# Two rows of a sample to a partition, four 64x64 tiles, the residual in the matrices, output slots and half stores

## The chip, the cores and the metric

The kernel runs on one core of one Trainium2 chip. The time is that of one execution on the device, in microseconds (us). Before the change it is 323.08 us, the median of three runs (323.06 to 323.25).

## What is computed

Each of 128 samples is a matrix of 128 channels by 1024 steps (float32, 512 KB). It is multiplied by the one of eight 128x128 matrices that its subject index names, and added to the product.

```python
B, C, D, T, N_SUBJECTS = (128, 128, 128, 1024, 8)
...
w = weights[subjects]
out = jnp.einsum('bct,bcd->bdt', x, w)
...
x = x + _L0_cond_ref(x, itok_B_0_7, L0_cond_weights)
```

67 MB come in, 67 MB go out, and everything is float32.

## The kernel before

A *turn* is four samples, two *halves* (`H`) of two samples (`G`); there are 32 turns. Twelve slots in SBUF (`xs`, pieces of `x_all`) hold one turn each: channel c of a sample stands in partition c, 4 KB of it, and the four samples stand side by side, 16 KB in a partition. A slot is loaded, overwritten with the sums, and stored.

The work is written for each engine by hand, between semaphores:

- **ACT's queue** issues the loads (`load`, through `transfer`, L67), one for each sample. `ROWS` = 4 makes the reading side one run of four rows, 16 KB; the writing side is four pieces of 4 KB in four partitions. A load waits only until its slot is stored (`s_slot`); the twelfth waits until the weights are sorted, since its slot holds them at first.
- **SP's queue** loads the weights (L192) and the indices (L195), then issues the stores (L251 for turn 0, `store` through L67 for the others). A store takes a whole turn from 128 partitions, 16 KB each; in the output these are four rows of 4 KB. The last twelve turns are stored in pairs (`PAIR`), the last six in runs of 32 KB (`WHOLE`). A store waits for the sums of its turn (`s_added`), and between turns `EARLY` = 8 and 24 for those of `BEHIND` = 4 turns more.
- **TensorE** runs a loop of 32 turns (`multiply`, L174): for each half four matmuls of 128x128 by 512 columns into that half's four banks of PSUM (`ps`). It waits for the two matrices (`s_go`) and for the landed samples (`s_ready`, L170). Ahead of the loop three matmuls on zeros (`IDLE`, L200) fill the time.
- **VectorE** sorts the weights at the start (two transposes, L208 and L227, and twelve of the sixteen copies at L230). Its loop then waits for a half's products, adds them to the samples in the slot (`add`, L186, 128x2048), and copies the two matrices of the next turn into place (`place`, L165), at addresses from the subject indices, which it loads into registers once a turn (L154).
- **GpSimd** does four of the sorting copies (L230) and then turns landed loads into `s_ready`.

Of the kernel before, what the change touches and what calls it, by code (L numbers as in the profile page):

```python
# [30 lines left out]
G = 2  # L31
H = 2

N = 512

SLOTS = 12

P_SLOTS = 2

BEHIND = 4  # L40
# [4 lines left out]
PAIR = 2  # L45
WHOLE = 6

DMA = 16

SORTED = 18  # L50

IDLE = 3
# [28 lines left out]
def kernel(  # L81
# [10 lines left out]
    NT = B // (G * H)  # L92
# [4 lines left out]

    room = -(nc.sbuf_base + -nc.sbuf_base % 32) % ALIGN
    if room:
        sbuf("room", C, room // 4)  # L100
    x_all = sbuf("x_all", C, SLOTS * H * G * T)
    xs = [
        x_all[:, i * H * G * T : (i + 1) * H * G * T].rearrange("c (q t) -> c q t", t=T)
        for i in range(SLOTS)
    ]
    w_all = sbuf("w_all", C, S, D)
    w_raw, w_mid, w_late = (xs[SLOTS - 1][:, q, :] for q in range(3))
    ws = [sbuf(f"w{i}", C, 1, D) for i in range(H * G)]
    zeros = sbuf("zeros", C, N)
    given, near, wrap = (sbuf(name, 1, B, dtype=I32) for name in ("given", "near", "wrap"))  # L110
    index = sbuf("index", 1, B + H * G, dtype=I32)
    ps = [
        ctx.enter_context(nc.psum_tensor(f"ps{i}", [D, G, T], F32)).ap() for i in range(P_SLOTS)
# [5 lines left out]
    s_zeros = tc.alloc_semaphore("s_zeros")  # L119
    s_product = tc.alloc_semaphore("s_product")  # L120
    s_added = tc.alloc_semaphore("s_added")

    s_ready = tc.alloc_semaphore("s_ready")
    s_go = tc.alloc_semaphore("s_go")

    s_slot = [tc.alloc_semaphore(f"s_slot{k}") for k in range(SLOTS)]
    s_head = tc.alloc_semaphore("s_head")
    s_sort = tc.alloc_semaphore("s_sort")

    def emptied(i):  # L130
        turns = i // SLOTS
        return DMA * (H * G + 1) * turns - (DMA * G if i >= SLOTS and i % SLOTS == 0 else 0)

    def load(engine, i, q):
# [17 lines left out]

    def subjects_of(i):
        _, subject = nc.values_load_multi_w_load_instructions(  # L154
            index[0:1, i] if isinstance(i, slice) else index[0:1, bass.ds(i * (H * G), H * G)],
            engines=[mybir.EngineType.DVE],
            min_val=0,
            max_val=S - 1,
            skip_runtime_bounds_check_because="the index is clamped on the chip above",
        )  # L160
        return subject

    def place(h, subject):
        for q in range(h * G, (h + 1) * G):
            copy = nc.vector.tensor_copy(ws[q], w_all[:, bass.ds(subject[q], 1), :])  # L165
        copy.then_inc(s_go, 1)

    def multiply(slot, h):
        nc.tensor.wait_ge(s_go, 1).then_inc(s_go, -1)
        nc.tensor.wait_ge(s_ready, 1).then_inc(s_ready, -1)  # L170
        for q in range(h * G, (h + 1) * G):
            for t in range(0, T, N):
                at = slot * (H * G * T) + (q * T + t)
                mm = nc.tensor.matmul(  # L174
                    ps[h][:, q % G, t : t + N],
                    ws[q][:, 0, :],
                    x_all[:, bass.ds(at, N)],
                    start=True,
                    stop=True,
                )  # L180
        mm.then_inc(s_product, 1)

    def add(slot, h):
        mine = x_all[:, bass.ds(slot * (H * G * T) + h * G * T, G * T)]
        nc.vector.wait_ge(s_product, 1).then_inc(s_product, -1)  # L185
        nc.vector.tensor_tensor(  # L186
            mine, ps[h].rearrange("d g t -> d (g t)"), mine, ALU.add
        ).then_inc(s_added, 1)

    with tc.tile_critical():  # L190

        nc.sync.dma_start(  # L192
            w_raw, weights.rearrange("s (u j) d -> (s u) (j d)", j=S)
# [5 lines left out]
        for _ in range(IDLE):  # L199
            nc.tensor.matmul(  # L200
                ps[P_SLOTS - 1][:, G - 1, :N], zeros[:, :D], zeros, start=True, stop=True
            )

        nc.vector.wait_ge(s_wall, DMA)
        nc.vector.transpose(  # L208
            w_mid.rearrange("p (e h w j) -> p j h e w", e=S, h=4, w=4), w_raw
        ).then_inc(s_sort, 1)  # L210
        nc.vector.memset(index[:, B:], 0).then_inc(s_index, 1)  # L211
# [5 lines left out]
        nc.vector.tensor_tensor(index[:, :B], near, wrap, ALU.add).then_inc(s_index, 1)  # L217
        for i in range(NT):
            if i == SLOTS - 1:
                nc.scalar.wait_ge(s_sort, SORTED)  # L220
            if i >= SLOTS:
                nc.scalar.wait_ge(s_slot[i % SLOTS], emptied(i))
            for q in range(H * G):
                load(nc.scalar, i, q)

        nc.vector.wait_ge(s_sort, 1)
        nc.vector.transpose(w_late, w_mid).then_inc(s_sort, 1)  # L227

        def sort(engine, o, v):
            engine.tensor_copy(  # L230
                w_all[32 * v : 32 * (v + 1), 2 * o : 2 * (o + 1), :],
                w_late[32 * o : 32 * (o + 1)].rearrange("c (e v d) -> c v e d", v=4, d=D)[:, v],
            ).then_inc(s_sort, 1)

        nc.vector.wait_ge(s_sort, 2)
        nc.gpsimd.wait_ge(s_sort, 2)
        for o in range(4):
            for v in range(4):
                sort(nc.gpsimd if v == 3 else nc.vector, o, v)
        for i in range(NT):  # L240
            if i == 0:
                nc.gpsimd.wait_ge(s_head, DMA * G).then_inc(s_ready, 1)
                nc.gpsimd.wait_ge(s_slot[0], DMA * G).then_inc(s_ready, 1)
            else:
                nc.gpsimd.wait_ge(s_slot[i % SLOTS], emptied(i) + DMA * H * G).then_inc(s_ready, H)

        for i in [*range(NT - SLOTS), *range(NT - SLOTS, NT, PAIR)]:
            n = 1 if i < NT - SLOTS else PAIR
            nc.sync.wait_ge(s_added, (i + n + (BEHIND if EARLY <= i < NT - LAST else 0)) * H)
            if i == 0:  # L250
                nc.sync.dma_start(  # L251
                    out[: H * G].rearrange("g d t -> d g t"), xs[0]
                ).then_inc(s_slot[0], DMA)
            elif i + n < NT:
                store(i, n).then_inc(s_slot[i % SLOTS], DMA)


        nc.vector.wait_ge(s_index, 4)
        nc.vector.wait_ge(s_sort, SORTED)
# [50 lines left out]
```

## Time and profile before

| | |
|---|---|
| time, median of three runs | 323.08 us |
| span of the profiled execution, first to last instruction | 320.9 us |
| moved by DMA | 134.76 MB, mean 420 GB/s |
| TensorE busy | 248.9 us, 78% |
| VectorE busy | 172.6 us, 54% |
| GpSimd busy | 1.9 us, 1% |
| mean granted TensorE clock | 0.893 |

The profiled execution has no time of its own beside its span; what lies around the span is taken as the difference to the runs' median. Times in the profile count from the start of the span. A row of the groups reads: line, engine, operation, output<-input, count, then busy time and the mean ns of one, then the engine's idle time just before them and what ended most of it. SPq and ACTq are the sequencers that issue DMAs. A busy TensorE is not TensorE at its peak, since its matmuls are pipelined and the records overlap.

### The profile page before, as it was taken

The numbers are of one execution on the slowest core, as the hardware profiler recorded it, in microseconds if no ns is written. First come the engines' busy times: TensorE is split into PE (matmuls) and PEld (weight loads), VectorE is DVE, ScalarE is ACT, GpSimd is POOL, SyncE is SP. The second block draws the span as 40 slices with busy tenths as digits, with TensorE's granted clock in tenths as the row PEclk, the third lists the DMA queues.
The fourth block names the chain that finished last, engine by engine and source line by source line (L and its number), as shares of the span: only waits on it lengthen the run. The fifth ranks groups of instructions, "written<-read, shape, count | busy, mean of one in ns | idle before, by whom it ended". The sixth has DMA issues, their size and how long they took to land. (4 is left out here: it accounts for less than half of the span.)

```text
span 320.9 us, 2386 instructions
## 1 busy us (share of the span) xinstructions
PE 248.9 (78%) x518; PEld 102.8 (32%) x518; DVE 172.6 (54%) x216; POOL 1.9 (1%) x8
## 2 busy tenths in 40 slices
PE   6199999999997699998498469988599957874000
PEld 2134444444433244443133224333244422331000
DVE  4636776777676167775435362675367745066000
POOL 0200000000000000000000000000000000000000
PEclk9679999999999599999789797999799989599555
DMA  7999999999999999999999999999999999999996
GB/s 294 425 425 412 426 423 432 429 423 425 425 425 425 425 424 425 425 429 425 429 435 431 427 427 429 425 425 425 425 425 425 425 425 425 427 427 455 429 445 274
DMA packets 10803, 134.76 MB, mean 420 GB/s; under 512 B 2481, under 2 KB 2482, under 8 KB 3122
## 3 DMA queue, kind: packets, MB, share of 16 engines
q1 hardware_dynamic: 4658, 67.64, 49.7%
q10 hardware_dynamic: 6144, 67.12, 49.6%
q14 instruction: 1, 0.01, 0.0%
HBM read 67.63 MB, written 67.11 MB: 420 GB/s over the span
## 5 line engine op out<-in xcount | busy, mean ns | idle before, releaser
L174 PE MATMUL ps<-x_all,w 128*128 x512 | 243.8, 635 | 42.0 <-PEq L170 34.3
L186 DVE TENSOR_TENSOR x_all<-ps,x_all 128x2048 f32 x64 | 146.7, 2292 | 117.3 <-DVEq L185 117.3
L174 PEld LDWEIGHTS ps<-x_all,w 128*128 128x128 f32 x512 | 100.9, 203 | 185.2 <-issue 184.6
L165 DVE COPY w<-w_all 128x128 f32 x132 | 23.2, 219 | 0.8 <-DVE w_all L230 0.8
L200 PE MATMUL ps<-zeros 128*128 128x512 f32 x6 | 5.2, 1033 | 1.7 <-DVE zeros L197 1.7
L230 DVE COPY w_all<-x_all 32x256 f32<-32x256 f32 x12 | 3.9, 326 | 0.4
L208 DVE STREAM_TRANSPOSE x_all<-x_all 128x1024 f32<-128x1024 f32 x1 | 2.0, 1992 | 3.1 <-DMA x_all<-in_L_cond_weights_dram 3.1
L200 PEld LDWEIGHTS ps<-zeros 128*128 128x128 f32 x6 | 1.8, 328 | 3.7 <-issue 2.1
L230 POOL COPY w_all<-x_all 32x256 f32<-32x256 f32 x4 | 1.7, 425 | 8.3 <-DVE x_all L227 8.1
L227 DVE STREAM_TRANSPOSE x_all<-x_all 128x1024 f32<-128x1024 f32 x1 | 1.2, 1225 | 0.0
L197 DVE MEMSET zeros<- 128x512 f32 x1 | 0.5, 485 | 1.0 <-SPq L190 1.0
L217 DVE CUSTOM_DVE_ANT_0 index<-near,wrap 1x256 uint16<-1x256 uint16 x1 | 0.3, 280 | 0.0
L215 DVE TENSOR_SCALAR wrap<-near 1x128 int32<-1x128 int32 x1 | 0.2, 215 | 0.0
L213 DVE TENSOR_SCALAR near<-given 1x128 int32<-1x128 int32 x1 | 0.2, 205 | 0.0
L297 POOL MEMSET const-bfloat16-1.0<- 128x1 bf16 x1 | 0.1, 100 | 0.0
L297 POOL MEMSET const-float32-0.0<- 128x1 f32 x1 | 0.1, 98 | 0.2 <-issue 0.2
L297 POOL MEMSET const-uint8-127<- 128x1 uint8 x1 | 0.1, 98 | 0.0
L297 POOL MEMSET const-float32-1.0<- 128x1 f32 x1 | 0.1, 97 | 0.0
L297 DVE BASE_LOAD x1 | 0.0, 21 | 0.1
L211 DVE MEMSET index<- 1x4 int32 x1 | 0.1, 62 | 0.0
## 6 DMA issues: line engine op xcount, KB each, us to landing
x_all<-in_x_dram ACTq DMA_DIRECT2D x128, 512.0 KB, 34.2
out_dram<-x_all SPq DMA_DIRECT2D x20, 2048.0 KB, 18.3
out_dram<-x_all SPq DMA_DIRECT2D x6, 4096.0 KB, 30.3
x_all<-in_L_cond_weights_dram SPq DMA_DIRECT2D x1, 512.0 KB, 3.7
given<-in_itok_B_dram SPq DMA_DIRECT2D x1, 0.5 KB
```

The costliest lines, as they stand in the source:

```text
L165: copy = nc.vector.tensor_copy(ws[q], w_all[:, bass.ds(subject[q], 1), :])
L174: mm = nc.tensor.matmul(ps[h][:, q % G, t : t + N], ws[q][:, 0, :], x_all[:, bass.ds(at, N)], start=True, stop=True,)
L186: nc.vector.tensor_tensor(mine, ps[h].rearrange("d g t -> d (g t)"), mine, ALU.add).then_inc(s_added, 1)
L197: nc.vector.memset(zeros, 0.0).then_inc(s_zeros, 1)
L200: nc.tensor.matmul(ps[P_SLOTS - 1][:, G - 1, :N], zeros[:, :D], zeros, start=True, stop=True)
L208: nc.vector.transpose(w_mid.rearrange("p (e h w j) -> p j h e w", e=S, h=4, w=4), w_raw).then_inc(s_sort, 1)
L213: nc.vector.tensor_scalar(near, given, -S, S - 1, ALU.max, ALU.min).then_inc(s_index, 1)
L215: nc.vector.tensor_scalar(wrap, near, 0, S, ALU.is_lt, ALU.mult).then_inc(s_index, 1)
L217: nc.vector.tensor_tensor(index[:, :B], near, wrap, ALU.add).then_inc(s_index, 1)
L227: nc.vector.transpose(w_late, w_mid).then_inc(s_sort, 1)
L230: engine.tensor_copy(w_all[32 * v : 32 * (v + 1), 2 * o : 2 * (o + 1), :], w_late[32 * o : 32 * (o + 1)].rearrange("c (e v d) -> c v e d", ...
L297: nc = _bacc.Bacc("TRN2", target_bir_lowering=False, num_devices=1)
```

## The change

*Layout.* A sample now takes 64 partitions with two of its rows in each, 8 KB, and two samples fill the 128 partitions. A turn is still four samples: two such pairs (`P`), each of two samples (`H`).

*Loads.* One load brings a pair: 64 runs of 16 KB on the reading side, two pieces of 8 KB each on the writing side. There are four input slots (`IN`), and a load waits until the sums of the turn four before it are copied out (`s_added`).

*Products.* A matrix is split by even and odd rows and columns into four 64x64 parts. A product is 32 calls of 64x64 by 512 columns, in four blocks `b` of eight; four calls in a row have their four tiles (`tile`: input rows `h`, output partitions `h ^ p`) in different quarters of the array. The identity (`same`, made by two selects on GpSimd) is added to each matrix as it is placed, so the product is the sum already. Both pairs together fill PSUM; blocks 0 and 2 write its first half, 1 and 3 the second. Blocks 0 and 1 wait until their half is copied out (`s_free`).

*Sums.* VectorE copies the products, a pair and a half of PSUM at a time (128x1024), into eight output slots (`OUT`). It waits for a free one (`s_room`), which GpSimd signals from the stores. Matrices are placed two turns ahead, into two sets.

*Stores.* By the crossing of tiles, partitions 0 to 63 of an output slot hold samples 0 and 3 of the turn, and 64 to 127 samples 1 and 2. So each half of the partitions is stored by itself: 64 runs of 16 KB, two pieces of 8 KB each in the output. `BEHIND` is 3.

*Start.* The weights are loaded by ACT's queue, ahead of the samples, 1 KB at a time into 64 partitions; one copy on VectorE and two parts of another, on VectorE and GpSimd (`SHARE` = 6 of 8), sort them. There are five matmuls on zeros.

On TensorE, the loop over turns before, with the waits (`ps` is PSUM, `w` the placed matrices; the ISA rows set an address):

```order
6 L174 ISA [waits s_go,s_ready]
7 L174 MATMUL ps<-x_all,w 128x512
8 L174 ISA
9 L174 MATMUL ps<-x_all,w 128x512
10 L174 ISA
11 L174 MATMUL ps<-x_all,w 128x512
12 L174 ISA
13 L174 MATMUL ps<-x_all,w 128x512
14 L174 ISA [waits s_go,s_ready]
```

And after, the first turn of the four in the loop's body and the start of the next:

```order
6 L192 MATMUL ps<-x_in,w 64x512 [waits s_go,s_ready,s_free]
7 L192 MATMUL ps<-x_in,w 64x512 x7
8 L192 MATMUL ps<-x_in,w 64x512 [waits s_free]
9 L192 MATMUL ps<-x_in,w 64x512 x23
10 L192 MATMUL ps<-x_in,w 64x512 [waits s_go,s_ready,s_free]
```

A turn's eight calls have become 32 smaller ones, the address rows are gone, and the two waits by half a turn have become one for landed data and two for free PSUM.

On VectorE, one turn of the loop before:

```order
23 L154 TENSOR_LOAD index
24 L186 ISA [waits s_product]
25 L186 TENSOR_TENSOR x_all<-ps,x_all 128x2048
26 L165 ISA
27 L165 COPY w<-w_all 128x128
28 L165 ISA
29 L165 COPY w<-w_all 128x128
30 L186 ISA [waits s_product]
```

And one turn after:

```order
29 L157 TENSOR_LOAD index
30 L204 ISA [waits s_room,s_product]
31 L204 COPY x_out<-ps 128x1024
32 L204 ISA
33 L204 COPY x_out<-ps 128x1024
34 L204 ISA [waits s_product]
35 L204 COPY x_out<-ps 128x1024
36 L204 ISA
37 L204 COPY x_out<-ps 128x1024
38 L168 ISA
39 L168 TENSOR_TENSOR w<-w_all,same 64x256
```

The additions have become copies, all four placements of a turn now stand behind its last copy, and a wait for an output slot stands in front.

On ACT's queue, the loads before:

```order
2 L67 DMA x_all<-in_x_dram 128x1024 x44
3 L67 DMA x_all<-in_x_dram 128x1024 [waits s_sort]
4 L67 DMA x_all<-in_x_dram 128x1024 x3
5 L67 DMA x_all<-in_x_dram 128x1024 [waits s_slot0]
6 L67 DMA x_all<-in_x_dram 128x1024 x3
```

And after:

```order
2 L67 DMA x_out<-in_L_cond_weights_dram 64x8x256
3 L67 DMA x_in<-in_x_dram 128x2048 x8
4 L67 DMA x_in<-in_x_dram 128x2048 [waits s_added]
5 L67 DMA x_in<-in_x_dram 128x2048
6 L67 DMA x_in<-in_x_dram 128x2048 [waits s_added]
```

44 loads of a sample went out without a wait, 22 MB; now it is the weights and eight loads of a pair, 8.4 MB, and each further turn waits for sums.

The core of the diff:

```diff
-SLOTS = 12
-P_SLOTS = 2
-BEHIND = 4
+IN = 4
+OUT = 8
+BEHIND = 3
...
-IDLE = 3
+IDLE = 5
+SHARE = 6
...
-    def store(i, n):
-        at = i % SLOTS * H * G * T
+    def load(i, p):
+        at = (i % IN * P + p) * SIZE
+        first = i * Q + p * H
         transfer(
             nc,
-            engine,
-            xs[i % SLOTS][:, q, :],
-            x[i * H * G + q].rearrange("(a r) t -> a (r t)", r=ROWS),
-        ).then_inc(s_head if i * H * G + q < G else s_slot[i % SLOTS], DMA)
+            nc.scalar,
+            x_in[:, at : at + SIZE],
+            x[first : first + H].rearrange("h (b r) t -> (h b) (r t)", r=ROWS),
+        ).then_inc(s_in[i % IN], DMA)
+    def store(i, h):
+        at = i % OUT * P * SIZE
+        first, step = (i * Q + h, Q - 1 - 2 * h)
         return transfer(
             nc,
             nc.sync,
-            out[i * H * G : (i + n) * H * G].rearrange("g d t -> d g t"),
-            x_all[:, at : at + n * H * G * T].rearrange(
-                "d (o t) -> d o t", o=1 if i >= NT - WHOLE else n
-            ),
+            out[first : first + step + 1 : step].rearrange("p (a r) t -> a p (r t)", r=R),
+            x_out[h * A : (h + 1) * A, at : at + P * SIZE].rearrange("a (o f) -> a o f", o=1),
         )
...
+    def place(u, subject):
+        return [
+            nc.vector.tensor_tensor(
+                ws[u][p][h * A : (h + 1) * A],
+                w_all[h * A : (h + 1) * A, bass.ds(subject[p * H + h], 1), :],
+                same[h * A : (h + 1) * A],
+                ALU.add,
+            )
+            for p in range(P)
+            for h in range(H)
+        ]
+    def multiply(i):
         nc.tensor.wait_ge(s_go, 1).then_inc(s_go, -1)
         nc.tensor.wait_ge(s_ready, 1).then_inc(s_ready, -1)
+        for b in range(BANKS):
+            if b < BANKS // 2:
+                nc.tensor.wait_ge(s_free, 1).then_inc(s_free, -1)
+            for r in range(R):
+                for p in range(P):
+                    for h in range(H):
+                        bank = b * 2 % BANKS + (b * 2 // BANKS + h) % 2
+                        e, t = divmod(bank * N, T)
+                        rows = slice(h * A, (h + 1) * A)
+                        cols = slice((h ^ p) * A, ((h ^ p) + 1) * A)
+                        at = (i % IN * P + p) * SIZE + r * T + t
+                        mm = nc.tensor.matmul(
+                            ps[p][cols, bank],
+                            ws[i % 2][p][rows, 0, r * D + e * A : r * D + (e + 1) * A],
+                            x_in[rows, at : at + N],
+                            start=r == 0,
+                            stop=r == R - 1,
+                        )
+            if b >= BANKS // 2:
+                mm.then_inc(s_product, 1)
...
+        transfer(
+            nc,
+            nc.scalar,
+            w_raw.rearrange("a (s f) -> a s f", s=S),
+            weights.rearrange("s (a r) d -> a s (r d)", r=R),
         ).then_inc(s_wall, DMA)
...
+        for i in range(NT):
+            if i >= IN:
+                nc.scalar.wait_ge(s_added, i - IN + 1)
+            for p in range(P):
+                load(i, p)
...
+        nc.gpsimd.wait_ge(s_zeros, 1).then_inc(s_room, OUT)
         for i in range(NT):
+            if i >= OUT:
+                nc.gpsimd.wait_ge(s_out[i % OUT], DMA * H * (i // OUT)).then_inc(s_room, 1)
+            nc.gpsimd.wait_ge(s_in[i % IN], DMA * P * (i // IN + 1)).then_inc(s_ready, 1)
...
+            nc.sync.wait_ge(s_added, i + 1 + (BEHIND if EARLY <= i < NT - LAST else 0))
+            for h in range(H):
+                if (i, h) != (NT - 1, H - 1):
+                    store(i, h).then_inc(s_out[i % OUT], DMA)
...
+        with nc.vector.Fori(0, NT // 2) as turn:
+            for u in range(2):
+                subject = subjects_of(bass.ds(turn * (2 * Q) + (u + 2) * Q, Q))
+                slot = (turn * 2 + u) % OUT
+                nc.vector.wait_ge(s_room, 1).then_inc(s_room, -1)
+                for half in range(2):
+                    nc.vector.wait_ge(s_product, 1).then_inc(s_product, -1)
+                    for p in range(P):
+                        copied = copy(slot, p, half)
+                    copied.then_inc(s_free, 1)
+                placed = place(u, subject)
+                placed[0].then_inc(s_added, 1)
+                placed[-1].then_inc(s_go, 1)
```

More of the change, by code (lines that the diff above doesn't have):

```diff
@@ new lines, in copy, with sort @@
+    def copy(slot, p, half):
+        at = slot * (P * SIZE) + (p * SIZE + half * T)
+        return nc.vector.tensor_copy(
+            x_out[:, bass.ds(at, T)],
+            ps[p][:, half * (T // N) : (half + 1) * (T // N)].rearrange("d b n -> d (b n)"),
+        )
+    def sort(engine, h, first, last):
+        engine.tensor_copy(
+            w_all[h * A : (h + 1) * A, first:last].rearrange("c s (r e a) -> c (s r) e a", r=R, e=R),
+            w_raw[:, first * R * D : last * R * D].rearrange(
+                "c (g a e) -> c g e a", a=D // R, e=R
+            ),
+        ).then_inc(s_sort, 1)
```

166 lines of the change are left out of this document (62 added, 104 removed).

## The prediction, made before the result

> **What bounds the kernel now.** The page comes first: which engine, if any, is full from end to end.
>
> ```profile
> span 320.9 us, 2386 instructions
> ...
> PE 248.9 (78%) x518; PEld 102.8 (32%) x518; DVE 172.6 (54%) x216; POOL 1.9 (1%) x8
> ...
> PEclk9679999999999599999789797999799989599555
> DMA  7999999999999999999999999999999999999996
> ...
> DMA packets 10803, 134.76 MB, mean 420 GB/s; under 512 B 2481, under 2 KB 2482, under 8 KB 3122
> ...
> q1 hardware_dynamic: 4658, 67.64, 49.7%
> q10 hardware_dynamic: 6144, 67.12, 49.6%
> ```
>
> No compute engine is full; the DMA engines are, in 38 of 40 slices (queue 1 is SP's, queue 10 ACT's). The second view is the busy time by stretches: length, the engines, granted clock, DMA share, GB/s.
>
> ```profile
> 0.00:4.00 4.00, 2.33 (x3) 1.17 (x4) 0.51 (x2) 0.20 (x4) 1.00 0.50 158
> 4.00:24.00 20.00, 12.29 (x20) 4.66 (x18) 10.82 (x25) 1.70 (x4) 0.74 1.01 427
> 24.00:284.00 260.00, 227.19 (x481) 94.00 (x480) 153.66 (x181) 0.00 (x0) 0.93 1.01 426
> 284.00:320.90 36.90, 7.13 (x16) 2.96 (x16) 7.63 (x9) 0.00 (x0) 0.67 0.94 402
> ```
>
> From 4 us on the 16 DMA engines have no free time: 134.76 MB at 426 GB/s is 316.3 us, and what is left of the 320.9 is the first few us and the end. The third view, the waits, asks whether compute matters anywhere.
>
> ```profile
> PE ps L174 <- PEq L170: 34.3, 12, 4.6
> ```
>
> TensorE waits twelve times for landed loads (its sequencer, L170), up to 4.6 us each. The end of the timeline says the same:
>
> ```profile
> 292.81 2.29 DVE L186 TENSOR_TENSOR x_all<-ps,x_all 128x2048 f32 x1 [0.81 <-DVEq L185]
> ...
> 295.69 0.54 SPq L67 DMA_DIRECT2D out_dram<-x_all  x1
> ```
>
> The last sum is done at 295 us, the last store is issued at 295.7, and 25 us of pure stores follow. So the time is bytes over DMA rate, plus an edge at each end. A change gains only by a cheaper packet or a shorter edge, and loses as soon as the DMA queues run dry.
>
> **What a packet costs.** Three answers on the DMA queues, in order: 290 to 310 us (stores alone, 32 KB packets), 60 to 110 us (both directions, 16 KB), and 2.6 to 3.6 us (the weights, 4 KB).
>
> ```profile
> q1 hardware_dynamic: 294, 8.49, 99.5%
> ...
> q1 hardware_dynamic: 825, 11.96, 56.3%
> q10 hardware_dynamic: 840, 9.29, 44.0%
> ...
> q1 hardware_dynamic: 79, 0.32, 81.7%
> ```
>
> Packets times their time is the share of 16 engines. 32 KB: 259 packets in 318.4 us, 1229 ns each, 615 per 16 KB. 16 KB: 730 in 450.4 us, 617 ns. 4 KB: 79 in 13.1 us, 165 ns, 660 per 16 KB. Two 16 KB packets made into one save about 4 ns; four 4 KB packets made into one save 43, 14 for each join. Loads and stores cost alike. In all three a packet is in 4 KB pieces on its finer side (a row of x or out, or of the slot). After the change a packet is still 16 KB, but in two pieces of 8 KB. No row has an 8 KB piece. Bounds: a piece costs nothing by itself, or as much as a packet's start: 4 ns by the nearest row (the large packets), 14 by the far one. Two pieces fewer then save 0 to 8 ns, at the far end 28; 28 would mean 445 GB/s, and no long stretch passes 429. I take 5 of 617, and 0 to 8 for the range. Each engine has (4096 + 4096) / 16 = 512 such packets: **-2.6 us** (0 to -4.1).
>
> The Trainium skill bears on this ("DMA: Bandwidth & Descriptors", "Where 436 GB/s comes from"): it puts the ceiling at 435 GB/s, by which 16 KB alone would take 602 ns. If all of the other 15 ns lay on the four pieces, an estimate from that page is 7.5 ns and 3.8 us saved.
>
> **The other terms.** *Completions.* Each transfer ends in a small packet on each engine: 2481 small ones is 155 transfers x 16, and one. After: 64 loads, 64 stores, weights and indices, 130. On queue 10 above, 567 packets x 617 ns leave about 2 us of its 352 for 273 small ones, 8 ns each: 25 x 8 = **-0.2 us**. *Tail.* 384 packets of 32 KB become 768 of 16 KB: 24 joins lost per engine x 4 ns = **+0.1 us**. *Head.* The timeline to the first product:
>
> ```profile
> 0.96 0.41 SPq L192 DMA_DIRECT2D x_all<-in_L_cond_weights_dram  x1
> ...
> 1.67 5.16 PE L200 MATMUL ps<-zeros 128*128 128x512 f32 x6 [1.67 <-DVE zeros L197]
> ...
> 4.71 1.99 DVE L208 STREAM_TRANSPOSE x_all<-x_all 128x1024 f32<-128x1024 f32 x1 [3.10 <-DMA x_all<-in_L_cond_weights_dram]
> ...
> 13.63 0.63 DVE L165 COPY w<-w_all 128x128 f32 x4 [0.85 <-DVE w_all L230]
> ...
> 14.54 2.07 PE L174 MATMUL ps<-x_all,w 128*128 x2 [7.71 <-DVE w L165]
> ```
>
> Weights come first on the engines today too (8 packets of 165 ns each), so x starts near 4 us. Afterwards they stand on ACT's queue ahead of x as 32 pieces of 1 KB per engine. Their price is not in the trace: 617/16 = 39 ns of data and a start of 4 to 14 gives 43 to 53, 1.4 to 1.7 us, against 1.3. Their issue, with four times the pieces, may hold x back further. Between 0 and +1.5 I take **+0.4 us**, near the row.
>
> **Does compute keep the queues full?** A turn of four samples moves 4.19 MB, 9.85 us at 426 GB/s. The price of compute needs the groups, then two weight loads in the warm stream:
>
> ```profile
> L174 PE MATMUL ps<-x_all,w 128*128 x512 | 243.8, 635 | 42.0 <-PEq L170 34.3
> L186 DVE TENSOR_TENSOR x_all<-ps,x_all 128x2048 f32 x64 | 146.7, 2292 | 117.3 <-DVEq L185 117.3
> L165 DVE COPY w<-w_all 128x128 f32 x132 | 23.2, 219 | 0.8 <-DVE w_all L230 0.8
> L230 DVE COPY w_all<-x_all 32x256 f32<-32x256 f32 x12 | 3.9, 326 | 0.4
> L230 POOL COPY w_all<-x_all 32x256 f32<-32x256 f32 x4 | 1.7, 425 | 8.3 <-DVE x_all L227 8.1
> ...
> 150.14 0.19 PEld L174 LDWEIGHTS ps<-x_all,w 128*128 128x128 f32 x1 [0.24 <-issue]
> 150.57 0.19 PEld L174 LDWEIGHTS ps<-x_all,w 128*128 128x128 f32 x1 [0.24 <-issue]
> ```
>
> 256 calls leave 512 records: each f32 call is two passes, 0.43 us apart when warm. After, a turn has 32 calls on 64x64 tiles, 64 passes. With four tiles at once: 16 x 0.43 = 6.9 us, in four blocks of 1.72. No row shows small tiles; the bounds are 6.9 (all four), 13.7 (two), 27.5 (one). I take 6.9: the four calls in a row sit in four different quarters of the array.
>
> On VectorE a copy of 1024 elements out of PSUM is not in the trace either: half of L186's 2292 ns is 1.15 us, at best half of that. I take 1.15. A placement with the identity (256 elements): 219 ns from below, 2292/8 = 287 from above, so 0.3. A turn is 4 x 1.15 + 4 x 0.3, with registers about 6.6 us.
>
> The new wait is s_free: block 0 waits for the first half of PSUM, block 1 for the second. Queued behind it on TensorE is the whole turn, and VectorE waits for that. The loop: block 2 ends, its two copies run to +2.5, the other half's to +4.9, then blocks 1 and 2 of the next turn: 4.9 + 2 x 1.72 = 8.3 us. That is under 9.85, so DMA still sets the pace; if copies were twice as fast, more so. GpSimd now also waits for the store of eight turns ago ahead of each "landed" signal, and nothing near that age is still in the store queue while stores are three turns late.
>
> **The start** has the thinnest cover. Only four slots take loads: 4.3 + 4 x 4.92 = 24 us, and then the queues are empty unless turn 0 is copied out. Weights land about 5; VectorE sorts 2560 elements (326/256 = 1.27 ns each: 3.3 us) while GpSimd sorts 1536 (425/256: 2.6 us). The two selects on GpSimd come before and have no row: at 0.4 us from the POOL copy or several times that, they fit into the 3 us in which it waits for weights. Then 0.7 us of index work, 0.9 to the first placement and 1.2 for four: TensorE starts near 11 us, against 14.5 now. One warm turn, copies and a placement: 11 + 6.9 + 2.8 + 0.3 = 21; with 1 to 2 us from issue to first packet, 23. Cover: 1 us. The clock decides:
>
> ```profile
> 9.00:20.00 11.00, 5.46 (x7) 2.35 (x8) 4.10 (x15) 1.25 (x4) 0.54 1.01 429
> 20.00:40.00 20.00, 20.00 (x47) 8.40 (x46) 14.06 (x16) 0.00 (x0) 1.00 1.00 416
> ```
>
> After an idle stretch of 7.7 us the first products ran at clock 0.54. Five warm-up matmuls instead of three (10 passes, the cold ones 0.86 us) reach to 8.5 or later, so the gap is 2 to 3 us and I expect a warm start. A wholly cold turn costs 6.9 more and leaves the queues empty for some 5 us. I put **+0.3 us** (0 to +5). At the end the stores held back (3 turns, 15 us) cover the last turn's 10 us: 0.
>
> **Sum.** The profiled execution has 320.9 us of span, and the runs' median is 323.1, so 2.2 lie around it: 320.9 + 2.2 - 2.6 - 0.2 + 0.1 + 0.4 + 0.3 = 321.1, say **321.2 us**. With the bounds of packets and head, 318.8 to 322.4 is this case.
>
> **Rivals.** *1. The pieces were never a cost.* Then 0 stands in place of -2.6: 323.7, from 322.4 to 324.8 with the head. For it: three packet sizes within 0.4% per byte at 16 KB and above. Against: the joins do save something.
>
> *2. The tiles overlap, but not fully.* With a step s in place of 0.43 the loop is 4.9 + 8s. It outruns the DMA when 11 + 10 for turn 0, 31 loops and 5 for the last store pass 319 us: loop 9.4, s = 0.57 (three tiles' worth at once). At s = 0.6, 327 + 3.5 = 330; a little above that, or with a cold first turn, 325 to 346.
>
> *3. Half the partitions store at half the rate.* A store now reads 64 partitions, all its packets the same half. While loads run beside it an engine gives stores only half its time, and half a rate suffices. Where stores run alone (284 to 319.6 today, 35.6 us, and about as long afterwards) it decides: double is +35 us, **356 us**; each 1% of rate lost there is 0.36 us, so above 5% the gain is gone and the change ends slower. For it: every transfer of the trace that has a rate spans all 128 partitions, so none shows that half of them suffice. Against: stores cost the same alone (615 ns) as beside loads (617), so the slots' side shows no limit of its own so far. The Trainium skill has the rule ("SBUF — State Buffer", "Door 1: The DMA port swizzle"): partitions 0 to 63 reach only 8 of 16 ports, 196 GB/s measured against 328 for all. No run here shows it yet.
>
> *4. The four tiles are not at once.* A call's two passes stand one behind the other on one tile. If passes start strictly in order, the second waits for the first and holds the next tile, so two run together: 13.7 us a turn, 439 + 11 + 10 + 3.5 = **463 us**. For it: the loads above start 0.43 us apart, never closer. Against: on one tile they could not. The Trainium skill ("TensorE: Matmul & The Clock Gate", "The mechanism" under packing) says that matmuls start and end in strict order, yet shows four row tiles 4 ns apart; it has no two-pass case.
>
> **Chances.** Forecast 0.45; rival 1 0.15; rival 2 0.20; rival 3 0.12; rival 4 0.08. About 0.2% is what a measurement here can tell from no change (322.4 to 323.7). Faster: the forecast, 0.45. Same: two thirds of rival 1, 0.10. Slower: the rest, 0.45. Signs are mixed, so the likeliest case's own range, 318.8 to 322.4, stands beside the full one: 318.8 to 346 takes in rivals 1 and 2 and leaves out 3 and 4, 0.20.
>
> **What would show it.** Right: the DMA row of nines throughout; 16 KB packets near 612 ns in the mixed stretch; weight loads four to a step of 0.43 us; no empty slice near 24 us. Wrong: 617 ns (rival 1); a TensorE row full with gaps in the DMA row (2 and 4, told apart by how many passes share a step); packets near 1200 ns where stores run alone (3).

## The result, and the profile after

The changed kernel takes 356.75 us (median of four runs, 355.24 to 361.81), against 323.13 for the kernel before on the same chip: a ratio of 1.1025 [1.0991, 1.106]. That is 33.6 us slower; the forecast was 321.2, and the range ended at 346. The profiled execution, from which places and packet times below are read, was the longest of the four, with a span of 360.0 us where the others have 353.5 to 356.0, and the ratio, which leaves it out, stands for 33.1 us.

The page, for the same lines as before (engines, DMA in tenths and GB/s in 40 slices of 9 us, packets, queues):

```profile
span 360.0 us, 5257 instructions
...
PE 255.6 (71%) x2058; PEld 93.3 (26%) x2058; DVE 208.9 (58%) x272; POOL 3.5 (1%) x7
...
DMA  7978999999999989999999999999999999999972
GB/s 242 428 320 288 365 393 382 402 386 393 391 382 419 370 320 395 364 393 395 390 402 411 406 400 406 393 400 404 408 393 400 408 407 406 400 339 377 390 300 106
DMA packets 10775, 134.81 MB, mean 374 GB/s; under 512 B 2065, under 2 KB 2578, under 8 KB 2578
...
q1 hardware_dynamic: 5122, 67.11, 49.5%
q10 hardware_dynamic: 5648, 67.64, 45.9%
```

The same bytes move at 374 GB/s in place of 420, and no compute engine is full. The row to look at is not DMA but GB/s: the engines are busy nearly all the time, and yet move 400 where they moved 427. So the packets themselves take longer. The busy time by stretches (length, engines, granted clock, DMA share, GB/s) separates this from a second loss:

```profile
24.00:27.00 3.00, 2.24 (x20) 0.84 (x24) 2.97 (x4) 0.00 (x0) 1.00 0.23 98
27.00:30.00 3.00, 3.00 (x32) 1.28 (x28) 1.27 (x4) 0.00 (x0) 1.00 0.57 98
...
130.00:140.00 10.00, 8.25 (x76) 2.90 (x72) 7.50 (x10) 0.00 (x0) 1.00 0.87 306
140.00:300.00 160.00, 122.43 (x1024) 44.82 (x1020) 102.08 (x132) 0.00 (x0) 0.94 1.00 399
...
330.00:340.00 10.00, 0.00 (x0) 0.00 (x0) 2.83 (x6) 0.00 (x0) 0.66 1.00 397
340.00:350.00 10.00, 0.00 (x0) 0.00 (x0) 0.00 (x0) 0.00 (x0) 0.50 0.76 318
350.00:360.00 10.00, 0.00 (x0) 0.00 (x0) 0.00 (x0) 0.00 (x0) 0.50 0.29 124
```

Two stretches have idle engines, at 24 to 30 us and at 130 to 140. At the end of this execution the engines finish one after another, for some 15 us. Everywhere else the share is full and the rate is low. Which packets are slow is told by the queues, from 10 to 20 us (loads alone) and from 60 to 110 us (both directions):

```profile
q10 hardware_dynamic: 332, 4.31, 100.9%
...
q1 hardware_dynamic: 742, 9.75, 54.6%
q10 hardware_dynamic: 747, 9.73, 46.0%
```

Loads alone: 161.4 us of engine time for 263 packets of 16 KB, 612 ns each after the small ones; before it was 617. Beside stores: loads (queue 10) 368 us for 594 packets, 620 ns; stores (queue 1) 437 us for 595, **about 732 ns**. This is a mean of two kinds: in the trace half of these store packets took 611 ns, a quarter more than 644, and a tenth more than 1160. So some stores are slow, and they are slow beside loads.

In the warm stream compute did nearly what was forecast. The groups (busy, mean ns of one | idle), and a piece of the timeline in the warm stream:

```profile
L192 PE MATMUL ps<-x_in,w 64*64 64x512 f32 x2048 | 249.2, 632 | 70.7 <-PEq L183 62.1 <-DVE w L168 5.3 <-DVE x_out L204 3.3
L204 DVE COPY x_out<-ps 128x1024 f32 x128 | 147.8, 1217 | 113.9 <-DVEq L292 113.9
...
L168 DVE TENSOR_TENSOR w<-w_all,same 64x256 f32<-64x256 f32 x136 | 57.1, 420 | 4.0 <-issue 1.0
```

```profile
150.27 0.18 PEld L192 LDWEIGHTS ps<-x_in,w 64*64 64x64 f32 x4 [0.25 <-issue]
150.70 0.18 PEld L192 LDWEIGHTS ps<-x_in,w 64*64 64x64 f32 x4 [0.25 <-issue]
```

Four weight loads stand in each step of 0.43 us: four tiles run at once.

### The profile page after: what moved, and what is told of

It is laid out like the page before. It is cut to its first block, busy times and chain, and to the rows that moved or that the text cites. A ratio compares the mean times of both kernels' runs of the same rounds, so it can differ in the third digit from the quotient of the medians.

```text
span 360.0 us, 5257 instructions
## 1 busy us (share of the span) xinstructions
PE 255.6 (71%) x2058; PEld 93.3 (26%) x2058; DVE 208.9 (58%) x272; POOL 3.5 (1%) x7
## 5 line engine op out<-in xcount | busy, mean ns | idle before, releaser
L192 PE MATMUL ps<-x_in,w 64*64 64x512 f32 x2048 | 249.2, 632 | 70.7 <-PEq L183 62.1
L204 DVE COPY x_out<-ps 128x1024 f32 x128 | 147.8, 1217 | 113.9 <-DVEq L292 113.9
L192 PEld LDWEIGHTS ps<-x_in,w 64*64 64x64 f32 x2048 | 90.7, 142 | 229.0 <-issue 228.9
L168 DVE TENSOR_TENSOR w<-w_all,same 64x256 f32<-64x256 f32 x136 | 57.1, 420 | 4.0 <-issue 1.0
L230 PE MATMUL ps<-x_out 128*128 128x512 f32 x10 | 6.4, 806 | 1.7 <-DVE x_out L227 1.7
L210 DVE COPY w_all<-x_out 64x2048 f32<-64x2048 f32 (+1 forms) x2 | 2.9, 1432 | 4.9 <-DMA x_out<-in_L_cond_weights_dram 4.8
L230 PEld LDWEIGHTS ps<-x_out 128*128 128x128 f32 x10 | 2.6, 268 | 4.7 <-issue 3.0
L210 POOL COPY w_all<-x_out 64x1536 f32<-64x1536 f32 x1 | 2.5, 2495 | 3.7 <-DMA x_out<-in_L_cond_weights_dram 3.7
```

Source lines behind the costliest of these rows:

```text
L168: nc.vector.tensor_tensor(ws[u][p][h * A : (h + 1) * A], w_all[h * A : (h + 1) * A, bass.ds(subject[p * H + h], 1), :], same[h * A : (h + ...
L192: mm = nc.tensor.matmul(ps[p][cols, bank], ws[i % 2][p][rows, 0, r * D + e * A : r * D + (e + 1) * A], x_in[rows, at : at + N], start=r == ...
L204: return nc.vector.tensor_copy(x_out[:, bass.ds(at, T)], ps[p][:, half * (T // N) : (half + 1) * (T // N)].rearrange("d b n -> d (b n)"),)
L210: engine.tensor_copy(w_all[h * A : (h + 1) * A, first:last].rearrange("c s (r e a) -> c (s r) e a", r=R, e=R), w_raw[:, first * R * D : la ...
L230: nc.tensor.matmul(ps[P - 1][:, BANKS - 1], zeros[:, :D], zeros, start=True, stop=True)
```

## The experiments

Three theories stood: **A**, stores of 64 partitions crowd one side of the partitions; **B**, the idle stretches, and what follows them, are the loss; **C**, the 8 KB pieces are slow at the output.

### One store of all partitions

```diff
-            out[first : first + step + 1 : step].rearrange("p (a r) t -> a p (r t)", r=R),
-            x_out[h * A : (h + 1) * A, at : at + P * SIZE].rearrange("a (o f) -> a o f", o=1),
+            out[i * Q : (i + 1) * Q].rearrange("(p h) (a r) t -> (h a) p (r t)", p=P, r=R),
+            x_out[:, at : at + P * SIZE].rearrange("a (o f) -> a o f", o=1),
```

> The changed kernel with one store a turn from all 128 partitions in place of two halves; in two of a turn's four samples the stored data then land in each other's place, nothing else differs. Theory A (a store from half the partitions is what costs): the slow packets go, all 16 KB packets take about 611 ns, and what is left of the loss are the two dry stretches near 24 and 130 us: 323 to 328 us. Theory B (the two dry stretches and the engines falling out of step after them): 350 us or more. Theory C (8 KB pieces at the output are slow): 352 to 358 us as before.

Measured: 332.62 us (331.81 to 333.31), 1.0302 [1.0274, 1.0329]. From 60 to 110 us:

```profile
DMA packets 1569, 21.53 MB, mean 431 GB/s; under 512 B 255, under 2 KB 255, under 8 KB 255
q10 hardware_dynamic: 875, 11.49, 53.8%
q1 hardware_dynamic: 694, 10.04, 47.0%
```

Stores take 376 us for 613 packets: 613 ns in place of 732, at the full rate of both queues. The half stores cost 356.75 - 332.62 = **24.1 us** by the medians, 23.4 by the two ratios, and C is out: the output is still written in pieces of 8 KB. The time lies above A's 323 to 328 us, so more is left beside the half stores than the two dry stretches were thought to cost.

### Halves in the kernel before, and which halves

The reverse: the kernel before, with the stores of turns 1 to 27 cut in two.

```diff
+        for rows in (slice(0, 64), slice(64, 128)):
+            store(i, n, rows).then_inc(s_slot[i % SLOTS], DMA)
...
-                store(i, n).then_inc(s_slot[i % SLOTS], DMA)
+                stores(i, n)
```

> The kernel before, with its stores (all but the first and the last two) cut into two halves of the partitions, 0 to 63 and 64 to 127. Theory A: mean store packets go from 616 to about 700 ns as in the changed kernel, and the time to 345 to 355 us. Theories B and C: nothing but 28 more completions of 16 packets, 323 to 324 us.

> As the run with halves in the kernel before, same targets and sizes, but both halves read partitions 32 to 95 (so the data are wrong). If the cost is that 0 to 63, or 64 to 127, are one side of the partitions (the port map of the Trainium skill has 32 to 63 and 64 to 95 on different ports): 323 to 324 us and packets of 616 ns. If any store from 64 partitions costs, by its number of partitions or of transfers: 345 to 355 us like the halves.

The reading side alone changes; the two halves of the output are written as in the first run:

```diff
+            x_all[slice(32, 96) if halved(i) else rows, at : at + n * H * G * T].rearrange(
```

> The kernel before, with the stores of its whole middle stretch cut into two transfers of 64 partitions as in the earlier run with 0 to 63 and 64 to 127 (364.6 us), but both transfers read partitions 0 to 63, so the second half of the output holds other data. A (what costs is that all engines read one side of the partitions at a time): there is no other side that an engine could go on to, so the loss is as large as with the two halves or larger: 360 to 430 us, 16 KB store packets at 750 ns or more, 32 KB ones at 1500 ns or more, loads near 630 ns. If the loss had come from the change between two sides, or from two transfers where there was one: this kernel never changes sides, and would take 323 to 330 us, as the one with partitions 32 to 95 did (323.4). C says nothing of it, since no piece is changed.

```diff
+            x_all[slice(0, 64) if halved(i) else rows, at : at + n * H * G * T].rearrange(
```

> The kernel before, with the stores of turns 1 to 27 cut in two as in the run of 364.6 us, but into the even and the odd partitions in place of the lower and the upper 64; the output is the reference's. A (which partitions the engines read at a time decides): each transfer takes 32 partitions of either side, so no side is crowded: 323 to 325 us, 16 KB store packets at 616 ns, 32 KB ones at 1228 ns. If two transfers of 64 partitions a turn cost by themselves, or partitions with a gap do: 340 us or more.

```diff
+        for rows in (slice(0, 128, 2), slice(1, 128, 2)):
```

Measured, with the GB/s of the three stretches below:

| partitions of the two stores | us | ratio | 50 to 280 | 280 to 310 | 310 to 340 |
|---|---|---|---|---|---|
| 0 to 63, then 64 to 127 | 364.63 | 1.1258 [1.1208, 1.1308] | 397 | 261 | 274 |
| 32 to 95, twice | 323.4 | 1.0012 [1.0003, 1.0022] | 426 | 428 | ends |
| 0 to 63, twice | 377.71 | 1.1708 [1.1689, 1.1726] | 380 | 339 | 224 |
| even, then odd | 326.77 | 1.0114 [1.01, 1.0129] | 421 | 431 | ends |

Queue 1 where stores run alone: with lower and upper halves at 290 to 310 us (beside 28 load packets), with 32 to 95 at 286 to 300 us (its last stores, behind that, are whole), and with 0 to 63 twice at 320 to 340 us.

```profile
q1 hardware_dynamic: 319, 4.70, 96.2%
```

```profile
q1 hardware_dynamic: 273, 6.05, 101.4%
```

```profile
DMA packets 232, 4.31 MB, mean 215 GB/s; under 512 B 32, under 2 KB 32, under 8 KB 32
q1 hardware_dynamic: 232, 4.31, 104.2%
```

The engines are full in all three, and move 235, 432 and 215 GB/s. So neither the number of transfers nor that of partitions decides, but which ones: 64 partitions that lie half below 64 and half above move at the full rate, and those on one side at half of it. The Trainium skill states this map ("SBUF — State Buffer", "Door 1: The DMA port swizzle": bit 6 of the partition picks one of two sets of eight ports), and the runs agree, at 215 to 432 where the page has 196 to 328. Lower and upper halves cost more than A's 345 to 355 us; beside loads, from 60 to 110 us, their packets took 692 ns (465 us for 670), and the stretches from 280 us on lose besides. That the even and odd partitions cost 3.7 us, above what was expected, stays open; from 60 to 110 us that kernel moves 426 GB/s, and from 100 to 250 us 415 to 419.

### Halves beside loads alone

```diff
     def halved(i):
-        return 0 < i < NT - 2 * PAIR
+        return 0 < i < NT - SLOTS
```

> The kernel before, with the stores of turns 1 to 19 alone cut into partitions 0 to 63 and 64 to 127; these run beside loads, and all later ones, that with the end of the program in which stores run alone, stay whole. The recorded rival (half a rate is enough for stores while loads take the other half, so halves cost only where stores run alone): 323 to 324 us, store packets of the halved turns near 616 ns. A as the runs so far have it (halves cost beside loads too): in the run with all of turns 1 to 27 halved (364.6 us) the transfers made some 395 GB/s between 50 and 280 us in place of 426, which is 15 to 17 us, less the last third of these turns: 331 to 341 us.

Measured: 344.25 us (343.12 to 347.98), 1.0695 [1.065, 1.0741]. The stretches 50 to 280 and 280 to 310 us of this kernel, whose stores from turn 20 on are whole again, and the first of them in the kernel before:

```profile
50.00:280.00 230.00, 189.59 (x388) 78.05 (x387) 123.93 (x145) 0.00 (x0) 0.92 1.01 400
280.00:310.00 30.00, 19.14 (x40) 7.71 (x39) 14.34 (x18) 0.00 (x0) 0.94 1.02 432
```

```profile
50.00:280.00 230.00, 197.48 (x415) 81.68 (x414) 132.61 (x156) 0.00 (x0) 0.93 1.01 427
```

Where loads run beside them, 19 turns of half stores cost **21 us**; the recorded rival had nothing there. It is also more than the 331 to 341 us that A gave: 400 GB/s in place of 427 over 230 us is 14.5 us of it, and the rest falls behind that stretch. The eight further turns of the run with all halves cost another 20.

### The halves in two queues

```diff
+        todo = [(max(i - IN + 1, 0), 0, i) for i in range(NT)]
+        todo += [(i + 1 + (BEHIND if EARLY <= i < NT - LAST else 0), 1, i) for i in range(NT - 1)]
...
+        for needs, stores, i in sorted(todo):
...
+                store(i, 1, nc.scalar).then_inc(s_out[i % OUT], DMA)
...
-            for h in range(H):
-                if (i, h) != (NT - 1, H - 1):
-                    store(i, h).then_inc(s_out[i % OUT], DMA)
+            store(i, 0).then_inc(s_out[i % OUT], DMA)
```

> The changed kernel with the store of partitions 64 to 127 issued on ACT's queue, among the loads, in place of SP's, so that both halves of a turn stand in queues of their own and can be in flight at once. A: an engine that serves both queues mixes the sides, and engines need no longer be on one side together; most of the 27 us of slow packets go, store packets at 612 to 650 ns, and the stores behind the last load run near 400 GB/s or more: 325 to 345 us (the dry stretches remain, and loads can wait behind stores that the order of the queue puts ahead of them). B alone: both dry stretches remain and nothing else changes, 350 to 358 us. C: the pieces remain, 350 to 358 us.

Measured: 365.17 us (362.91 to 368.67), 1.1342 [1.129, 1.1394]; every theory missed. Queues from 60 to 110 us:

```profile
q10 hardware_dynamic: 1204, 15.81, 80.1%
q1 hardware_dynamic: 342, 4.29, 20.4%
```

The lower half's stores, alone on queue 1, fall to 623 ns (163 us for 262 packets), but queue 10, with loads and upper halves, stands at 664 (641 us for 965). A queue for each half doesn't mend it. The Trainium skill says so ("SBUF — State Buffer", "Can I just issue two DMAs to hit both halves?": only 6% more for two at once); the run agrees that it is no remedy. What stands there too, that only one transfer over all 128 partitions reaches all ports, is not borne out: 32 to 95 moved at the full rate. From 50 to 280 us this kernel is no slower than the profiled execution of the changed one (397 GB/s against 392); it falls back after that (374 against 407 up to 310 us, 348 against 372 up to 340). Loads that wait behind stores in queue 10 would explain this, but no run shows it.

### The idle stretches

From here on with full stores, from 332.62 us.

```diff
-IN = 4
+IN = 8
-OUT = 8
+OUT = 4
-BEHIND = 3
+BEHIND = 0
```

> The changed kernel with one store of 128 partitions a turn (samples 1 and 2 of each turn land in each other's place), as in the earlier run of 332.6 us, and then 8 slots for x and 4 for the output in place of 4 and 8, and no store held back. B: the 9.5 us that the full stores leave above the kernel before are the two dry stretches (20 to 30 us and 120 to 130 us of that run) and the slow load packets right behind each (703 to 845 ns); with eight slots the queue of loads lasts past the first store, and with none held back there is no second gap: 319 to 324 us, DMA share 0.95 or more in every 10 us from 10 us on, load packets near 612 ns. If what is left is instead the cost of the loads' or the stores' new form in the steady state, it stays at 329 to 334 us with the rows of both stretches full.

```diff
-EARLY = 8
+EARLY = 6
...
-            nc.sync.wait_ge(s_added, i + 1 + (BEHIND if EARLY <= i < NT - LAST else 0))
+            nc.sync.wait_ge(s_added, i + 1 + (min(BEHIND, i // EARLY) if i < NT - LAST else 0))
```

> The changed kernel with one store of 128 partitions a turn (332.6 us in the earlier run; samples 1 and 2 of each turn land in each other's place), and the stores held back by one turn more from turns 6, 12 and 18 on, in place of three turns at once from turn 8. B: the gap at 120 to 130 us (DMA share 0.82 there, loads at 732 ns behind it) came from three stores held at once, which leaves the loads alone for three turns, and they can't go faster than slots come free, one turn of 2.1 MB in 8.8 us. Spread out, the gap goes for the most part: 1.8 us of idle engines and 1.8 us of slow packets less, 328 to 330 us; the stretch at 20 to 30 us stays. If the gap had another cause, it stays, and the time at 332 to 333 us.

Measured: 334.18 us (333.23 to 334.97), 1.0355 [1.0334, 1.0376], for eight input slots, and 330.0 us (329.92 to 330.09), 1.0217 [1.0202, 1.0231], for stores held back slowly. The first by stretches:

```profile
40.00:290.00 250.00, 195.88 (x1664) 72.66 (x1664) 164.86 (x210) 0.00 (x0) 0.97 1.01 428
290.00:304.00 14.00, 10.78 (x84) 4.04 (x85) 8.02 (x11) 0.00 (x0) 0.88 0.94 400
304.00:331.00 27.00, 12.67 (x112) 4.64 (x112) 14.12 (x20) 0.00 (x0) 0.80 0.57 242
```

With eight slots, and no store held back, both gaps are gone, but loads have run so far ahead that after the last one the stores can only follow compute, a turn (2.1 MB) in 8.76 us, 239 GB/s: the loss has moved to the end, and B's number missed. The second, with the stretches at both ends:

```profile
0.00:4.00 4.00, 2.33 (x3) 1.17 (x4) 0.51 (x3) 1.05 (x6) 1.00 0.28 75
4.00:10.00 6.00, 5.11 (x8) 1.72 (x6) 3.24 (x4) 2.51 (x1) 1.00 1.09 376
...
20.00:27.00 7.00, 5.55 (x52) 1.93 (x48) 5.87 (x7) 0.00 (x0) 1.00 0.72 302
27.00:40.00 13.00, 11.51 (x104) 4.12 (x96) 8.15 (x11) 0.00 (x0) 1.00 0.95 360
40.00:100.00 60.00, 50.00 (x440) 18.43 (x444) 42.74 (x56) 0.00 (x0) 1.00 1.01 430
...
322.00:324.00 2.00, 0.00 (x0) 0.00 (x0) 0.00 (x0) 0.00 (x0) 0.50 0.11 45
324.00:326.00 2.00, 0.00 (x0) 0.00 (x0) 0.00 (x0) 0.00 (x0) 0.50 0.06 25
```

The same places in the kernel before (its first 4 us, at 158 GB/s, are in the prediction):

```profile
4.00:10.00 6.00, 2.83 (x4) 0.67 (x2) 5.10 (x10) 1.30 (x3) 0.98 1.00 419
...
20.00:27.00 7.00, 7.00 (x18) 2.89 (x17) 4.93 (x6) 0.00 (x0) 1.00 1.01 428
27.00:40.00 13.00, 13.00 (x31) 5.50 (x30) 9.13 (x12) 0.00 (x0) 1.00 0.99 410
40.00:100.00 60.00, 59.59 (x136) 24.96 (x136) 42.84 (x52) 0.00 (x0) 1.00 1.01 427
```

The second gap is closed by holding back slowly, for 332.62 - 330.0 = **2.6 us**, as expected. The remaining 7.0 us over the kernel before lie in these rows. From 20 to 40 us (428 - 302) x 7 + (410 - 360) x 13 = 1532 KB are missing, 3.6 us of transfer at 428; up to 10 us (158 - 75) x 4 + (419 - 376) x 6 = 590 KB, 1.4 us; and from 322 us to the end at 328.1 hardly anything moves, since a few engines finish late (the kernel before has 2.9 us of that, from 318 us on). The steady 430 GB/s in place of 427 gives some 2 us of 280 back.

### The larger pieces by themselves

The kernel before, with two rows of a sample per partition on the load side alone: twelve slots and its own full stores stay. The products go by tiles of 64x128 in all four kernels; where a recorded text below has 64x64, that is a slip.

```diff
-            xs[i % SLOTS][:, q, :],
-            x[i * H * G + q].rearrange("(a r) t -> a (r t)", r=ROWS),
+            x_all[:, at : at + G * T],
+            x[first : first + G].rearrange("g (a r) t -> (g a) (r t)", r=ROWS),
```

Four kernels differ only in how the matrices come: in 1 KB pieces from SP's queue; the same from ACT's queue ahead of x; the same behind turn 0; and in 4 KB pieces from SP's queue, transposed on VectorE as before.

> A combination: the slots, queues and full stores of the kernel before, but loads with two rows of a sample in a partition (8 KB pieces), row tiles of 64x128, the identity in the matrices, and copies in place of additions. Theory A and the cheaper piece (611 for 616 ns): 256 load packets per engine save 1.3 us, 64 fewer loads 0.5, the weights in 1 KB pieces cost 0.2 to 0.6: 321.2 to 322.2 us. If small pieces were never a cost: 322.8 to 323.4. If row tiles do not overlap: 400 us or more.

> The kernel with two rows per partition on the load side alone (twelve slots, full stores of the kernel before, four 64x64 products at once, identity in the matrices; 325.3 us in the earlier run), with the load of the matrices put ahead of x on ACT's queue, where the changed kernel has it, in place of SP's queue. B (engines out of step at the start, because the packets of the matrices came between those of x on one queue, so that loads ran at 660 to 748 ns until 45 us): load packets at 612 ns from the start, the first store by 30 us, and 320 to 322 us, below the kernel before by the 4 ns that 4 KB pieces cost over 8 KB ones on the loads (4096 load packets of 16 KB over 16 engines, about 1 us) and by an earlier start of the stores. If loads alone write one side at a time and so run slow by themselves, as stores did: they stay near 700 ns until the stores begin, 324 to 326 us.

> The kernel with two rows per partition on the load side alone (324.05 us with the matrices first on ACT's queue), with the matrices behind the loads of turn 0 on that queue. With the matrices first, the DMA engines made 119 GB/s from 2 to 4 us and 307 from 4 to 6 us, where the kernel before made 315 and 422: some 1.5 us of lost transfer; from 30 us on it made 428 to 429 GB/s in place of 423 to 428. B: behind turn 0, their 512 packets of 1 KB (46 ns each in the middle) cost some 0.3 us and no more, as they come while the queue is full: 321.8 to 323.0 us, under the kernel before or level with it. If the packets of the matrices between those of x bring the engines into step as they did from SP's queue, loads run at 660 to 750 ns up to 45 us again: 324.5 to 326 us.

> The kernel with two rows per partition on the load side alone (324.05 and 324.25 us with the matrices in pieces of 1 KB on the queue of x), with the matrices fetched as the kernel before does it (4 KB pieces on SP's queue, two transposes of blocks on VectorE, 16 copies), so that the head of the transfers is that of the kernel before. B: its DMA makes some 420 GB/s from 4 us on, as before, and 428 GB/s in place of 426.5 once it runs in step with no gap, which over 290 us is 1 us: 321.8 to 322.4 us, below the kernel before. If the 4 ns a packet that the larger pieces save are lost elsewhere (an uneven end of the engines, as the 2 us between 318 and 320 us in the earlier runs): 322.7 to 324 us.

Measured, in this order: 325.25 us, 1.007 [1.0053, 1.0086]; 324.05 us, 1.003 [1.0017, 1.0042]; 324.25 us, 1.0053 [1.0034, 1.0072]; 322.81 us, 0.9992 [0.9983, 1.0001]. All four lie above what B or the cheaper piece was to give. The second lies in the range of its other case, but not for that reason: its loads take 611 ns from 20 us on, not near 700. The 4 to 20, 20 to 50 and 50 to 280 us of the first and of the last:

```profile
4.00:20.00 16.00, 3.16 (x4) 0.67 (x2) 0.00 (x0) 0.00 (x0) 0.71 1.02 384
20.00:50.00 30.00, 23.50 (x96) 11.12 (x96) 18.88 (x22) 1.06 (x1) 0.81 1.00 371
50.00:280.00 230.00, 200.21 (x870) 94.54 (x868) 172.78 (x167) 0.00 (x0) 0.97 1.01 428
```

```profile
4.00:20.00 16.00, 6.03 (x12) 2.30 (x12) 11.62 (x22) 2.85 (x4) 0.69 1.00 427
20.00:50.00 30.00, 28.57 (x130) 13.31 (x129) 23.42 (x22) 0.00 (x0) 0.99 1.00 420
50.00:280.00 230.00, 202.10 (x860) 95.03 (x856) 168.34 (x163) 0.00 (x0) 0.95 1.01 428
```

In the middle all gain what was forecast for half the packets, 428 over 427 GB/s. The head takes it away: the four ways of fetching 0.5 MB of matrices differ by 2.4 us. The best of them is 0.2 us under the kernel before, with an interval that reaches 1, and above the 321.8 to 322.4 that was expected. So 8 KB pieces are worth at most 0.2% there, and no version clearly beats the kernel before.

## Why the prediction was wrong

The step that failed stands in **rival 3**, where it says of stores beside loads that "an engine gives stores only half its time, and half a rate suffices"; on the strength of it the sum has nothing at all for half stores beside loads. The mechanism was named, with its source in the Trainium skill, but priced only where stores run alone. Halves beside loads alone cost 21 us in the kernel before; all half stores of the changed kernel cost 23.4. The mean need of one side is indeed half of what 16 engines ask. But the engines need not be spread evenly at each moment, and a store packet may meet too many others on its side. The traces from 60 to 110 us bear this out in part. In the changed kernel, of the store packets during which fewer than seven were under way on average, 6% take more than 650 ns; with eight or more it is 29%; with one full store a turn it is 0 or 1% at any number. But eight is no border: where all stores read partitions 0 to 63, it is 76% even below seven. How many engines on one side are too many stays open.

The number of that rival, 356, was met by luck. At the end, where it had put all 35 us, the changed kernel still moves 397 GB/s at 330 to 340 us, and 6% of its store packets take more than 1000 ns; the kernel before with the same halves moved 235 at 290 to 310, and it is 66%. The landings of the stores in the traces tell the two apart: in the kernel before all 16 engines finish a half within 3.1 us of each other, and a half takes them 9 us, so most of the time all of them read the same side. In the profiled execution of the changed kernel they are some 18 us apart, while both halves of a turn take an engine 4.9 us, so both sides are mostly being read at once. This fits, but no run sets the distance of the engines by itself.

Its chance of 0.12, and a range that left it out, were the mistake in weighing: no row of before showed a half store, and a rule that did stood beside it.

The other steps:

- **Pieces, -2.6 us**: the size was right for the packet (612 ns in place of 617), and the 430 GB/s of the run with slow holding back are worth some 2 us in the steady part. They never came out as time. (Rival 1 counts three packet sizes within 0.4%; the rows have two, 615 and 617 ns, and 660 for the third.)
- **Four tiles at once**: right, and rivals 2 and 4 are refuted, by four weight loads to a step of 0.43 us.
- **The loop, 8.3 us**: a copy took 1217 ns for 1150 and a placement 420 for 300; the second turn's copies begin 8.76 us after the first's (30.70 and 21.94, below). The DMA stays the slower one.
- **The stores held back, 0**: missed. Three held at once from turn 8 leave the loads alone to fill the queues, and with four slots they come at the pace of compute; this is the second gap, 2.6 us.
- **Head, +0.4 us**: 1.4 with full stores and the same head, since the first 4 us move 75 GB/s where they moved 158, and the next six 376 for 419.

**The start, +0.3 us (0 to +5)**: the cover of 1 us was not there. The timeline (start, length, engine, operation):

```profile
11.21 3.50 DVE L168 TENSOR_TENSOR w<-w_all,same 64x256 f32<-64x256 f32 x8 [1.04 <-issue]
...
13.39 9.91 PE L192 MATMUL ps<-x_in,w 64*64 64x512 f32 x64 [5.30 <-DVE w L168]
...
21.94 4.62 DVE L204 COPY x_out<-ps 128x1024 f32 x4 [7.23 <-DVEq L292]
...
27.03 1.40 SPq L67 DMA_DIRECT2D out_dram<-x_out  x2
...
30.70 3.48 DVE L204 COPY x_out<-ps 128x1024 f32 x3 [2.38 <-DVEq L292]
```

TensorE started at 13.4, not near 11, and its first turn took 9.9 us, not 6.9, after it had idled for 5.3; in the run with full stores held back slowly, with the same start, the granted clock was 0.83 from 10 to 20 us. So turn 0 is out at 27, where 21 was forecast; the loads that this sets free move from 28.3 on, while the queue was empty at 24. The store is issued at 27 too, but its first packet moves at 32.0: 5 us from issue to packet, where 1 to 2 were allowed. With what follows the gap this is 3.6 us in the run with full stores, inside the range that was given.

So by the ratios, of 33.1 us, 23.4 are the half stores, 2.7 the stores held back at once, and 7.0 the start, the head and the late engines, less what the pieces give.

## What to carry to other kernels

When a layout puts a result into half of the partitions, look at which half each transfer reads: here two transfers of 64 partitions came near one of 128 only where each lay on both sides of partition 64 (0.3 and 3.7 us more, against 41.5). Don't take a mean load that a resource can just carry as proof that it costs nothing; price such a rule everywhere that the resource is used, not only where it is used alone. And where DMA is the limit, take a sum for the first idle microsecond of its queues: stock in the input slots against the time of the first result.

## What the hardware showed that was not expected

- Loads over all partitions are slow too, for a while, right behind a gap, or when the packets of another transfer come between them: in the kernel with the matrices from SP's queue they move 384 and 371 GB/s up to 50 us with all engines busy, and 428 afterwards. The two are not alike: in that kernel eight in ten load packets from 25 to 40 us take 739 to 748 ns, while behind the second gap of the run with one full store a turn (120 to 130 us) half take 611 and a quarter over 1030. That engines in step write one side together was not tried by itself, and the cause of either is open.
- A few engines finish late once the flow has been disturbed: with stores held back slowly, the last 6 us pass at 45 GB/s and less.
